# A four-layer graph kernel: layer 3 in row chunks, loads from SyncE, sums moved between engines, another planned order

## The chip, the cores and the metric

The kernel runs on one core of a Trainium2 chip. Times are microseconds (us) of device time, from the program's start to its end on that core. The kernel before took 3013.47 us as the median of three runs (3012.79 to 3015.4). One further execution was taken by the hardware profiler; it took 3013.04 us, of which the profile's span (first to last instruction) is 3011.3 us.

The engines are PE (TensorE: matmuls and transposes), DVE (VectorE), ACT (ScalarE), POOL (GpSimd) and SP (SyncE). Each works through its own queue in order. SP does nothing here but start transfers (DMAs). POOL starts the transfers that add into their target.

## The reference

There are 32 graphs of 512 nodes, 256 features each, with a weighted adjacency matrix of 512 x 512. Each graph goes through four layers, and after each layer the features are added to the layer's result and normalised by row. All values are float32.

```python
x = norm(x + L0(x, adj))    # h = (1+eps)*x + adj@x ; relu(h@W1+b1)@W2+b2
x = norm(x + L1(x, adj))    # 4 heads: softmax(leaky_relu(e_dst+e_src), masked adj>0.5) @ h + bias
x = norm(x + L2(x, adj))    # 8 heads: softmax(q@k.T/sqrt(32) + log(adj+1e-6)) @ v, then @Wo.T+bo
x = norm(x + L3(x, mask, adj))  # softmax((x@W)@x.T * adj, masked nodes) @ x
```

## The kernel before

The work of one graph is cut into a few hundred named steps, each on one engine. A node's 512 rows are four chunks of 128 (`NC` = 4), the 256 features two (`DC` = 2). The names that matter below, in order of a graph's way:

- **Loads and layer 0.** SP starts the load of `x` (512 KB, step `ldx`) and then of the whole adjacency matrix `A` (1 MB, `ldA`). PE transposes `A` in 16 blocks, one output column block m at a time (`at`, L639), so each `at` step reads all four row chunks. ACT copies each to `AT` (`ate`, L647); DVE makes the diagonal blocks with 1+eps added, `ATd` (L643). Then `hT` (L671), `h1T` with W1 (L694), `y` with W2 (L713), the residual sum (L601), and the norm: two statistics per chunk on DVE (L559, L560), `ve` (L572), a power on POOL (`rstd`, L577), `shift` (L582), and one ACT pass per chunk (L590).
- **Layer 1.** `xT` (L739), values `v` (L760), then small exponentials `R`, `S`, `T`, `nT`. `R` is transposed (L799), copied to rows (L804), written to DRAM by SP (L809) and read back spread over all partitions as one 1 MB transfer `R_bc` (L811). ACT and DVE make the weights `z` from it (L850, L861). `o1` multiplies them with the values (L884), with 64-column tiles of the PE array. Column sums of the values for nodes without edges, `hs`, are four matmuls with one column each (L822). The sums of the weights over the nodes: POOL starts transfers that add the four chunks of each head's `z` together (L912, two after each other per head), then PE multiplies by ones with 32-column tiles, 128x512 (`d1`, L930). ACT copies the sum `dT` (L941), and PE transposes both halves of the result and `dT` per chunk (`yt`: L949, L950, L951). DVE takes four small reciprocals (L957) and divides (L959).
- **Layer 2.** `q`, `k`, `v` (L1009, L1027), scores for four heads at once in 32-row tiles (`s`, L1046), exponentials (L1059), times `AT` (L1068), product with the values in 32-column tiles (`n`, L1104). The sums go as in layer 1: transfers that add (L1079, three for each half of the heads, the last behind the other two), then ones (`d2`, L1128), copy (L1136), reciprocal (`rc`, L1143), product (`yd`, L1147), output projection `p` (L1176), norm.
- **Layer 3.** `A` is loaded again as one 1 MB transfer (L1190), `iT` (L1215), scores `s` (`t`, L1229), product with `A` (`ta`, L1243), masked maximum (`tb`, L1249), exponential (`te`, L1257), all into one tile `z`. The 16 transposes (`u`, L1274) each take one block of every row chunk's `z`. Then the copies (`ue`, L1283), the product with `x` (`w`, L1301), the sum (L1315), statistics, norm, and one 512 KB store (`out`, L1330).

The weights are loaded at the start from ACT's queue (L320), 15 transfers in all, ahead of ACT's first own instruction.

The order on every engine is written by a small planner, `Plan`, while the program is built. Each step has an engine, an estimated time, the steps it comes after and the buffers it takes (`take`) and gives back (`free`). `Plan.order` walks through time: of the steps that could start soonest it picks the one with the earliest due time. A step's due time is `max(g - 1, 0) * period - left`, where `left` is the estimated time from the step to its graph's end; `stay` adds a penalty for a change between PE's tile shapes (`mode`: none, 32-row, 32-column, 64-column), of the size in the table `CHANGE`; `moved` shifts the due times of the first and the last graph's steps at random by a seed. `run` tries three settings and emits the instructions of the best. Up to six graphs are open at a time, so PE always has steps of several graphs to pick from; once emitted, the order is fixed, and an engine waits wherever the next instruction in its queue isn't ready. SP's steps count 0.1 us, and each load has a queue name of its own (`q0`, `q2`, `q3`).

Of the kernel before, what the change touches and what calls it, by code (L numbers as in the profile page):

```python
# [17 lines left out]
P = 128  # L18
# [28 lines left out]
class Plan:  # L47
# [7 lines left out]

    HOP = {"pe": 0.2, "act": 0.15, "dve": 0.13, "pool": 0.05, "sp": 0.05}
# [3 lines left out]
        "": {"": 0.0, "row": 0.1, "c32": 0.1, "c64": 0.1},  # L60
        "row": {"": 0.13, "row": 0.1, "c32": 0.2, "c64": 0.2},
# [72 lines left out]
    def order(self, period, ahead, window, stay, shift=0.0, seed=0):  # L134
# [10 lines left out]
        rng = random.Random(seed)  # L145
        moved = {n: rng.uniform(-shift, shift) for n in [*self.steps[0], *self.steps[-1]]}
# [10 lines left out]
        while low < len(self.steps):  # L157
            found = []
            for (g, name), t in ready.items():
                s = self.steps[g][name]  # L160
                t = max(t, engine.get(s.eng, 0.0))
                change = self.CHANGE[mode][s.mode] if s.eng == "pe" else 0.0
                for k, (kind, _, rest) in enumerate(s.take):
                    r, n = room[kind], sum(b[0] == kind for b in s.take[:k])
                    if len(r) <= rest + n:
                        break
                    t = max(t, r[n][0])
                else:
                    due = max(g - 1, 0) * period - self.left[g][name] + moved[name] + stay * change
                    found.append((t, due, g, name, change))  # L170
# [46 lines left out]
def fast_path(  # L217
# [57 lines left out]
    wg_sb = const.tile([P, DC, VW], F32, name="wg_sb")  # L275
    ab_off = const.tile([P, 2, H1], F32, name="ab_off")
# [6 lines left out]
    def blk(i):  # L283
# [4 lines left out]
        "B": 14, "C": 13, "p": 8,  # L288

        "live": 6, "L0": 1, "L1": 2, "L2": 2, "L3": 1, "AT": 4, "zs": 7,  # L290
        "ATd": 1, "edge": 1, "dT": 1, "tmp": 2, "rdT": 2, "node": 1,
# [7 lines left out]
    def row(name, n):  # L299
        return tuple(f"{name}{i}" for i in range(n))  # L300


    def prepare():
# [10 lines left out]
        def load(name, us, *transfers, take=()):  # L314


            @step(f"ld_{name}", "act", 0.5 * len(transfers), take=take)
            def _():
                for transfer in transfers:
                    nc.scalar.dma_start(*transfer())  # L320

            @step(name, "q3", us, (f"ld_{name}",))
            def _():
                pass
# [4 lines left out]
        def transposed(name, w):  # L329
# [4 lines left out]
            load(f"raw{name}", 1.2, raw, take=(f"C=raw{name}",))  # L334
# [18 lines left out]
        load("eps", 2.0, lambda: (eps_bc, row_bcast(eps0, 1)))  # L353
# [3 lines left out]
        def _():  # L357
# [3 lines left out]
        load(  # L361
            "w1", 3.0, lambda: (w1_sb, rows(w1)), lambda: (b1_sb, b1.rearrange("(c p) -> p c", p=P))
        )
# [8 lines left out]
        load("bias", 3.0, *(bias_rows(k, b) for k, b in enumerate((b2, gbias, bo))))  # L372

        def vector(name, a):
# [6 lines left out]
        load(  # L381
            "wg", 3.0,
            lambda: (wg_sb[:, :, :D], wg.rearrange("(c p) h f -> p c (h f)", p=P)),
            vector("a0", a_src), vector("a1", a_dst), take=("C=a0", "C=a1"),
        )

        @step("wa", "dve", 3.2, ("wg",), take=("C=prod",), free=("prod", "a0", "a1"))
        def _():
            for k in range(2):
# [6 lines left out]
                )  # L396

# [125 lines left out]
    def graph(g):  # L523
        plan.graph()
        slot = plan.slot[-1]
        t = {"g": g}
# [4 lines left out]
        def mid(key, shape, name):  # L531
            return sb.tile(shape, F32, tag=f"C{slot[key]}", name=f"{name}_{g}")

# [24 lines left out]
        def norm_stats(n, c):  # L558
            nc.vector.bn_stats(t[f"st{n}"][:, c, :], t["x"][:, c, :])  # L559
# [6 lines left out]
        def norm_steps(n, after):  # L566


            @step(f"ve{n}", "dve", 0.09, after)
            def _():  # L570
                t["ve"] = little([P, NC], f"ve{n}")
                nc.vector.tensor_scalar_add(t["ve"], t[f"mv{n}"][:, :, 1], LN_EPS)  # L572

            @step(f"dev{n}", "pool", 1.1, (f"ve{n}",))
            def _():
                t["rstd"] = little([P, NC], f"rstd{n}")
                nc.gpsimd.tensor_tensor(t["rstd"], t["ve"], nhalf, ALU.pow)  # L577

            @step(f"sh{n}", "dve", 0.09, (f"dev{n}",))
            def _():  # L580
                t["shift"] = little([P, NC], f"shift{n}")
                nc.vector.scalar_tensor_tensor(  # L582
                    t["shift"], t[f"mv{n}"][:, :, 0], -1.0, t["rstd"], op0=ALU.mult, op1=ALU.mult
                )

            for c in range(NC):

                @step(f"r{n}{c}", "act", 0.49, (f"sh{n}",) + prev(f"r{n}", c))
                def _(c=c):
                    nc.scalar.activation(  # L590
                        t["x"][:, c, :], t["x"][:, c, :], AF.Identity,
                        bias=t["shift"][:, c : c + 1], scale=t["rstd"][:, c : c + 1],
                    )
# [17 lines left out]
        @step("ldx", "sp", 0.1, take=("live", "C=x/2"))  # L611
# [4 lines left out]
        @step("ldA", "sp", 0.1, ("ldx",), take=("L0", "B=A0/5"))  # L616
        def _():
            t["A"] = big("A0", [P, NC, N], "A")
            nc.sync.dma_start(t["A"], adj[g].rearrange("(c p) m -> p c m", p=P))

        @step("ld", "q0", 8.0, ("ldA",))
        def _():
            pass


        for m in range(NC):

            @step(
                f"at{m}", "pe", 0.44, ("ld",) + prev("at", m),
                take=(f"p=at{m}",) + (() if m else ("AT=ATcap", "B=AT/5", "ATd")),  # L630
            )
            def _(m=m):
                if m == 0:
                    t["AT"] = big("AT", [P, NC, N], "AT")

                    t["ATd"] = sb.tile([P, NC, P], F32, tag="ATd", name=f"ATd_{g}")
                pt = t[f"pt{m}"] = bank(f"at{m}", [P, N], f"AT_t_{m}")
                for c in range(NC):
                    nc.tensor.transpose(pt[:, blk(c)], t["A"][:, c, blk(m)], ident)  # L639

            @step(f"atd{m}", "dve", 0.2, (f"at{m}", "^selfw"))
            def _(m=m):
                nc.vector.tensor_add(t["ATd"][:, m, :], t[f"pt{m}"][:, blk(m)], selfw)  # L643

            @step(f"ate{m}", "act", 0.52, (f"at{m}",))
            def _(m=m):
                nc.scalar.copy(t["AT"][:, m, :], t[f"pt{m}"])  # L647

            plan.free(f"at{m}", (f"atd{m}", f"ate{m}"))
        plan.free("A0", row("at", NC))  # L650
        plan.free("L0", row("at", NC))

        for d in range(DC):

            @step(
                f"h{d}", "pe", 3.49, row("ate", NC) + row("atd", NC) + prev("h", d),
# [26 lines left out]
        for f in range(HC):  # L683

            @step(
                f"f{f}", "pe", 1.72, row("he", DC) + prev("f", f) + ("^w1",),
# [33 lines left out]
        norm_steps(1, row("st1", NC))  # L720
# [6 lines left out]
        for d in range(DC):  # L727
# [5 lines left out]
            def _(d=d):  # L733
                if d == 0:
                    t["xT"] = mid("xT1", [P, DC, N], "xT1")
                    t["xs"] = little([P, DC], "xs")
# [43 lines left out]
        def _():  # L780
            t["R"] = little([P, H1 * NC], "R")
            nc.scalar.activation(
                t["R"], t["ab"][:, 1].rearrange("p h c -> p (h c)"), AF.Exp, scale=1 - SLOPE
# [13 lines left out]
        def _():  # L797
            t["pr"] = bank("Rt", [P, P], "R_t")
            nc.tensor.transpose(t["pr"][: H1 * NC, :], t["R"], ident)  # L799

        @step("Re", "dve", 0.19, ("Rt",), free=("Rt",))
        def _():
            t["Rr"] = little([H1 * NC, P], "R_rows", 1)
            nc.vector.tensor_copy(t["Rr"], t["pr"][: H1 * NC, :])  # L804

        @step("Rd", "sp", 0.1, ("Re",), take=("B=R/4",))
        def _():
            R_dram = dram.tile([H1 * NC, P], F32, tag="R_dram", name=f"R_dram_{g}")
            nc.sync.dma_start(R_dram, t["Rr"])  # L809
            R_bc = t["Rbc"] = big("R", [P, H1, N], "R_bc")  # L810
            nc.sync.dma_start(R_bc.rearrange("p h n -> p (h n)"), row_bcast(R_dram, H1 * N))  # L811

        @step("Rl", None, 8.5, ("Rd",))
        def _():
            pass

        @step("hs", "pe", 0.9, row("xe1", DC) + ("^wa",), take=("p=hs",))
        def _():
            ph = t["phs"] = bank("hs", [P, DC], "hs_ps")
            for o in range(DC):  # L820
                for d in range(DC):
                    nc.tensor.matmul(  # L822
                        ph[:, o : o + 1], wg_sb[:, d, blk(o)], t["xs"][:, d : d + 1],
                        start=(d == 0), stop=(d == DC - 1),
                    )

        @step("hse", "act", 0.1, ("hs",), free=("hs",))
        def _():
            t["hs"] = little([P, DC], "hs")
            nc.scalar.mul(t["hs"], t["phs"], TINY)  # L830
# [12 lines left out]
        for h in range(H1):  # L843
            for c in range(NC):

                @step(f"z{h}{c}", "act", 0.7, ("Rl", "ST") + prev(f"z{h}", c), take=() if c else (f"B=z{h}",))
                def _(h=h, c=c):
                    if c == 0:
                        t[f"e{h}"] = big(f"z{h}", [P, NC, N], f"z1_{h}")
                    nc.scalar.activation(  # L850
                        t[f"e{h}"][:, c, :], t["Rbc"][:, h, :], AF.Relu,
# [14 lines left out]
        plan.free("R", tuple(f"z{h}{NC-1}" for h in range(H1)))  # L866


        for hp in range(H1 // 2):
            for k in range(2):  # L870
# [20 lines left out]
                f"oe{hp}", "act", 0.59, (f"o1{hp}1", "hse") + prev("oe", hp),  # L891
# [34 lines left out]
        @step("d1", "pe", 0.87, tuple(f"as{h}1" for h in range(H1)), take=("p=d1",), mode="c32")  # L926
        def _():
            t["pd"] = bank("d1", [P, N], "d1_ps")
# [885 lines left out]
```

## Time and profile before

| | |
|---|---|
| median of three runs | 3013.47 us |
| profiled execution | 3013.04 us |
| its span | 3011.3 us |
| PE busy | 2944.1 us (98%), 15053 matmul records |
| DVE, ACT, POOL busy | 2009.7 (67%), 1946.5 (65%), 619.8 us (21%) |
| DMA queue of the adding transfers (q0) | 62.0% of the 16 engines' span |
| DMA queue of SP (q1) | 13.8% |
| first matmul of layer 3's last product, graph 16 to graph 17 | 90.53 us apart, and the same for most neighbours |

A matmul of float32 leaves two records, a transpose one. The page's groups give the busy time and the mean latency of one record; matmuls overlap in the array, so what one costs PE's queue is read from the starts of the groups that follow each other in the timeline, not from the latency. A wait names what ended last before the instruction could start. The clock line gives the share of full speed that TensorE was granted.

### The profile page before, as it was taken

The page shows a single profiled execution, that of the slowest core. Times are in us where ns is not written, and L with a number is a line of the kernel's source. Part 1 is how long each engine was busy: PE and PEld are TensorE (multiplying, and loading weights), DVE is VectorE, ACT ScalarE, POOL GpSimd, SP SyncE. Part 2 cuts the span into 40 slices and gives each one's busy share as a digit, 9 for nine tenths or more (in the row PEclk, how much of TensorE's full clock was granted, in tenths as well). Part 3 has the DMA queues.
Part 4 walks back from the last instruction along what each step waited for, and adds up shares of the span by engine and source line. Part 5 has one row for each costly group of instructions (what it writes and reads, how often), then busy time and mean ns, then how long its engine had stood idle before and what let it go on. Part 6 is the DMA issues. An engine that isn't in the chain of part 4 may idle for free. (4 is left out here: it accounts for less than half of the span.)

```text
span 3011.3 us, 40812 instructions
## 1 busy us (share of the span) xinstructions
PE 2944.1 (98%) x15053; PEld 1703.7 (57%) x15053; DVE 2009.7 (67%) x3935; ACT 1946.5 (65%) x3849; POOL 619.8 (21%) x686
## 2 busy tenths in 40 slices
PE   7899999999999999999999999999999999999996
PEld 5544655555565555565555565555565555565544
DVE  1467576676676676676676676676676676676874
ACT  2667566767666767666767666767666767666762
POOL 0222122112222112222112222112222112222210
PEclk9999999999999999999999999999999999999998
DMA  4579767788887788887787887787877787887963
GB/s 152 125 173 194 154 137 172 160 180 177 180 168 165 161 182 174 180 166 170 160 184 171 181 166 168 160 187 168 180 163 173 160 189 168 177 168 150 199 133 79
DMA packets 159782, 500.82 MB, mean 166 GB/s; under 512 B 13132, under 2 KB 48728, under 8 KB 130904
## 3 DMA queue, kind: packets, MB, share of 16 engines
q0 software_dynamic: 78336, 352.36, 62.0%
q1 hardware_dynamic: 77824, 142.88, 13.8%
q10 hardware_dynamic: 3416, 2.90, 0.3%
q8 instruction: 121, 1.98, 0.3%
q14 instruction: 85, 0.70, 0.1%
HBM read 179.06 MB, written 17.05 MB: 65 GB/s over the span
## 5 line engine op out<-in xcount | busy, mean ns | idle before, releaser
L1068 DVE SCALAR_TENSOR_TENSOR z<-AT,z 128x1024 f32<-128x1024 f32 x512 | 610.9, 1217 | 273.2 <-ACT z L1059 272.7
L1059 ACT ACTIVATE z<-s 128x512 f32<-128x512 f32 x1024 | 551.3, 611 | 268.3 <-PE s L1046 268.1
L1143 DVE RECIPROCAL rdT<-rdT 128x256 f32<-128x256 f32 x128 | 218.3, 1728 | 316.2 <-ACT rdT L1136 316.2
L861 DVE SCALAR_TENSOR_TENSOR z<-z,T,edge 128x512 f32<-128x512 f32 x512 | 357.8, 747 | 62.2 <-ACT z L850 62.0
L850 ACT ACTIVATE z<-R_bc,nT,S 128x512 f32<-128x512 f32 x512 | 382.1, 819 | 17.8 <-DMA R_bc<-R_dram 17.8
L1079 POOL DMA_DIRECT2D z<-z x192 | 169.5, 883 | 992.2 <-PE o_ps L1104 268.7
L590 ACT ACTIVATE x<-x,shift,rstd 128x256 f32<-128x256 f32 x512 | 295.4, 602 | 108.0 <-DVE shift L582 108.0
L912 POOL DMA_DIRECT2D z<-z x256 | 228.8, 1033 | 467.5 <-DMA z<-z 265.2
L1046 PE MATMUL s<-qT,kT 32*128 32x512 f32 x2048 | 291.8, 634 | 0.1
L577 POOL TENSOR_TENSOR rstd<-ve,nhalf 128x4 f32<-128x4 f32 x128 | 134.7, 1052 | 696.9 <-DVE ve L572 671.6
L1104 PE MATMUL o_ps<-z,v 128*32 128x512 f32 x2048 | 260.5, 601 | 0.3 <-ACT z L1059 0.3
L694 PE MATMUL h1T_ps<-hT,w_sb 128*128 128x512 f32 x512 | 240.0, 604 | 0.0
L1229 PE MATMUL s<-xT,iT 128*128 128x512 f32 x512 | 237.4, 598 | 0.0
L1301 PE MATMUL o_ps<-x,eT 128*128 128x256 f32 x1024 | 237.4, 385 | 0.0
L713 PE MATMUL y_ps<-w_sb,h1T 128*128 128x256 f32 x1024 | 232.4, 381 | 2.2 <-ACT h1T L700 2.2
L884 PE MATMUL o_ps<-z,v 128*64 128x512 f32 x1024 | 230.8, 602 | 1.5 <-DVE z L861 1.5
L1301 PEld LDWEIGHTS o_ps<-x,eT 128*128 128x128 f32 x1024 | 189.5, 190 | 68.1 <-issue 22.8
L713 PEld LDWEIGHTS y_ps<-w_sb,h1T 128*128 128x128 f32 x1024 | 194.6, 191 | 52.8 <-issue 20.7
L671 PE MATMUL hT_ps<-AT,x 128*128 128x384 f32 (+2 forms) x768 | 210.1, 383 | 8.8 <-ACT AT L647 8.8
L559 DVE BATCH_NORM_STATS2 st<-x 128x6 f32<-128x256 f32 x512 | 211.9, 414 | 5.6
L1046 PEld LDWEIGHTS s<-qT,kT 32*128 32x128 f32 x2048 | 93.5, 183 | 158.7 <-issue 66.8
L694 PEld LDWEIGHTS h1T_ps<-hT,w_sb 128*128 128x128 f32 x512 | 90.5, 190 | 122.0 <-issue 112.8
(145 smaller groups left out, 4261.5 us busy)
## 6 DMA issues: line engine op xcount, KB each, us to landing
z<-z POOLq DMA_DIRECT2D x192, 1024.0 KB, 8.2
A<-in_adj_dram SPq DMA_DIRECT2D x64, 1024.0 KB, 11.0
z<-z POOLq DMA_DIRECT2D x128, 512.0 KB, 8.0
x<-biases POOLq DMA_DIRECT2D x96, 512.0 KB, 9.6
R_bc<-R_dram SPq DMA_DIRECT2D x32, 1024.0 KB, 4.5
z<-z POOLq DMA_DIRECT2D x128, 256.0 KB, 7.7
x<-in_x_dram SPq DMA_DIRECT2D x32, 512.0 KB, 6.0
out_dram<-x SPq DMA_DIRECT2D x32, 512.0 KB, 3.8
```

Of the source, the lines that this page charges most:

```text
L590: nc.scalar.activation(t["x"][:, c, :], t["x"][:, c, :], AF.Identity, bias=t["shift"][:, c : c + 1], scale=t["rstd"][:, c : c + 1],)
L694: nc.tensor.matmul(ph, w1_sb[:, d, blk(f)], t["hT"][:, d, :], start=(d == 0), stop=(d == DC - 1))
L713: nc.tensor.matmul(py[:, j, :], t["h1T"][:, f, blk(2 * c2 + j)], w2_sb[:, f, :], start=(f == 0), stop=(f == HC - 1),)
L850: nc.scalar.activation(t[f"e{h}"][:, c, :], t["Rbc"][:, h, :], AF.Relu, bias=t["nT"][:, h, c : c + 1], scale=t["S"][:, h, c : c + 1],)
L861: nc.vector.scalar_tensor_tensor(z, z, t["T"][:, h, c : c + 1], t["edge"][:, c, :], op0=ALU.add, op1=ALU.mult)
L884: nc.tensor.matmul(po[j * F1 : (j + 1) * F1, :], t["v"][:, c, h * F1 : (h + 1) * F1], t[f"e{h}"][:, c, :], start=(c == 0), stop=(c == NC - 1),
L1046: nc.tensor.matmul(pk, t["k"][hs, o, blk(c)], t["q"][hs, o, :], start=True, stop=True)
L1059: nc.scalar.activation(t[f"E{k}"][:, j, :], t[f"ps{k}{j}"], AF.Exp, scale=QSCALE)
L1068: nc.vector.scalar_tensor_tensor(z, t["AT"][:, c, None, :].to_broadcast([P, 2, N]), ADJ_EPS, z, op0=ALU.add, op1=ALU.mult,)
L1104: nc.tensor.matmul(t[f"n{o}"][32 * j : 32 * j + 32, :], t["v2"][:, c, o * P + F2 * j : o * P + F2 * (j + 1)], t[f"E{k}"][:, j, :], start=( ...
L1229: nc.tensor.matmul(pt, t["iT"][:, d, blk(c)], t["xT3"][:, d, :], start=(d == 0), stop=(d == DC - 1),)
L1301: nc.tensor.matmul(py[:, j, :], t["eT"][:, m, blk(2 * c2 + j)], t["x"][:, m, :], start=(m == 0), stop=(m == NC - 1),)
```

## The change

The change rewrites many steps and the settings of the planner. By part:

1. **Start.** `A` is loaded in four row chunks, ahead of `x`. `at` now takes one row chunk and writes one block column of `AT` (a strided copy). The large weights go to SP's queue behind the first graph's `A` and `x`; only `eps`, `b1`, the biases and `a_src`/`a_dst` stay with ACT.
2. **Layer 1.** `R_bc` becomes four transfers, one per head. The feature sums `xs` travel as two more columns of `R` through the same transpose and DRAM write, are read back by all partitions, and DVE makes `hs` from them with two reductions against a transposed `wg` (made once, `wtg`, `weg`). The four `hs` matmuls go. `d1` multiplies by `pick`, a 128x32 matrix with a column of ones at place c, 16 matmuls of 128 columns that leave the sums as [32h + c, node]; one transpose (`dt`) and one reciprocal (`rd1`) then serve all four chunks, and `yt` transposes two blocks instead of three.
3. **Layer 3 by row chunks.** `A`, `z` and `eT` become strips of 256 KB, and scores, mask, exponential, transpose, copy, product run chunk by chunk; the transposes of a chunk no longer wait for the other chunks.
4. **Last graph.** For graph 31 alone layer 2's sums are made by PE over all chunks (32 matmuls instead of 8, and no adding transfers), and the last norm and the store run per chunk. `yd` is split in halves for every graph.
5. **Planner.** SP's steps count 0.45 us and share a transfer queue `q1`; buffers are regrouped into 19 strips (`D`); `CHANGE` has other numbers; every step's due time can be shifted, by a list of seeds found beforehand; one setting is left.

```diff
-        "": {"": 0.0, "row": 0.1, "c32": 0.1, "c64": 0.1},
-        "row": {"": 0.13, "row": 0.1, "c32": 0.2, "c64": 0.2},
+        "": {"": 0.0, "row": 0.13, "c32": 0.1, "c64": 0.1},
+        "row": {"": 0.17, "row": 0.1, "c32": 0.2, "c64": 0.2},
...
+        for seed, far in shifts:
+            rng = random.Random(seed)
+            for n in moved:
+                if rng.random() < 0.15:
+                    moved[n] += rng.uniform(-far, far)
...
+    pick = const.tile([P, NC, 32], F32, name="pick")
+    nc.gpsimd.memset(pick, 0.0)
+    for c in range(NC):
+        nc.gpsimd.memset(pick[:, c, c : c + 1], 1.0)
...
+    def transfer(name, us, after, queue="q1"):
+        @step(f"{name}.q", queue, us, after)
+        def _():
+            pass
+        @step(name, None, 2.0, (f"{name}.q",))
+        def _():
+            pass
...
-                    nc.scalar.dma_start(*transfer())
+                    (nc.scalar if little else nc.sync).dma_start(*transfer())
...
+                t[f"A{c}"] = strip(f"A0{c}", [P, N], f"A{c}")
+                nc.sync.dma_start(t[f"A{c}"], adj[g].rearrange("(c p) m -> p c m", p=P)[:, c, :])
...
-                for c in range(NC):
-                    nc.tensor.transpose(pt[:, blk(c)], t["A"][:, c, blk(m)], ident)
+                for m in range(NC):
+                    nc.tensor.transpose(pt[:, m, :], t[f"A{c}"][:, blk(m)], ident)
...
-                nc.scalar.copy(t["AT"][:, m, :], t[f"pt{m}"])
+                nc.scalar.copy(t["AT"][:, :, blk(c)], t[f"pt{c}"])
...
-            nc.sync.dma_start(R_bc.rearrange("p h n -> p (h n)"), row_bcast(R_dram, H1 * N))
+                nc.sync.dma_start(t[f"R{h}"], row_bcast(t["Rdram"][h * NC : (h + 1) * NC, :], N))
...
-                    nc.tensor.matmul(
-                        ph[:, o : o + 1], wg_sb[:, d, blk(o)], t["xs"][:, d : d + 1],
-                        start=(d == 0), stop=(d == DC - 1),
-                    )
+                nc.vector.tensor_tensor_reduce(
+                    t["xsr"][:, 1, :], t["xsr"][:, 0, :], wgT[:, o, :], TINY, 0.0,
+                    op0=ALU.mult, op1=ALU.add, accum_out=t["hs"][:, o : o + 1],
+                )
...
-                nc.tensor.matmul(
-                    t["pd"][32 * h : 32 * h + 32, :], ones[:, :32], t[f"e{h}"][:, 0, :],
-                    start=True, stop=True,
-                )
+            for c in range(NC):
+                for h in range(H1):
+                    nc.tensor.matmul(
+                        t["pd"][32 * h : 32 * h + 32, :], pick[:, c, :], t[f"e{h}"][:, 0, blk(c)],
+                        start=(c == 0), stop=(c == NC - 1),
+                    )
...
-                nc.tensor.transpose(pt[:, 2, :], t["dT"][:, blk(c)], ident)
...
-            if c % 2:
+            if c % 2 and not last:
                 collect(k, k - 1, (f"n{k-1}", f"m{k}1"))
...
-            @step(f"u{m}", "pe", 0.44, row("te", NC) + prev("u", m), take=(f"p=u{m}",))
+            @step(f"u{c}", "pe", 0.44, (f"te{c}",) + prev("u", c), take=(f"p=u{c}",), free=(f"z3{c}",))
...
-        norm_steps(4, row("st4", NC))
+        norm_steps(4, [[c] for c in range(NC)] if last else [range(NC)])
...
-        plan.run([(28, 0.0, 6, 100.0, 8.0, 34035), (28, 0.05, 6, 30.0, 3.0, 427523), (28, 0.0, 6, 15.0)])
+        plan.run([(33, 0.0, 6, 55.0, ((619770, 10.0), ...), (0.7, 0.0, 0.0))])
```

In the order that comes out, PE's queue repeats from graph to graph as it did before, with 21 changes of tile shape per graph in both kernels. On POOL, the power of layer 2's norm of one graph now stands behind three of the four second adding transfers of layer 1 of the next graph but one. The last 35 groups of PE's queue mix graphs 30 and 31, and graph 31's layer 3 stands alone at the end.

## The prediction

> **What bounds the kernel now.** I read the page's busy shares first: PE 98%, no other engine over 67%. Then PE by stretches of the span, to see where the missing 2% lies (columns: stretch, its length, busy us of PE, of weight loads, DVE, ACT, POOL, clock, DMA share, GB/s).
>
> ```profile
> 0.00:11.60 11.60, 0.00 (x0) 0.03 (x1) 1.01 (x8) 0.00 (x0) 0.96 (x10) 1.00 0.76 249
> 11.60:32.47 20.87, 12.04 (x56) 10.20 (x57) 1.17 (x4) 3.92 (x6) 0.00 (x0) 1.00 0.81 277
> 470.00:2650.00 2180.00, 2179.93 (x11274) 1268.10 (x11275) 1504.18 (x2937) 1465.81 (x2894) 460.01 (x504) 1.00 0.79 171
> 2957.30:2998.70 41.40, 30.35 (x99) 18.57 (x100) 17.29 (x43) 12.39 (x25) 2.04 (x2) 0.84 0.04 13
> 2998.70:3011.30 12.60, 1.25 (x6) 0.76 (x4) 4.02 (x14) 2.07 (x4) 1.01 (x1) 0.70 0.14 46
> ```
>
> From 470 to 2650 us PE never waits: a graph takes 90.53 us there because its matmuls do. All 67.2 us in which PE is idle lie at the ends: 20.4 before 32 us, 17.3 more up to 470, 16.9 from 2841 to 2998.7, 12.6 after the last matmul. So only two things can move the time: fewer microseconds in PE's queue per graph (times 32), and shorter ends. PE's own waits (us in total, times, longest) and the timeline of ACT name the first gaps:
>
> ```profile
> PE AT_t L639 <- DMA A<-in_adj_dram: 11.6, 1, 11.6
> PE hT_ps L671 <- ACT AT L647: 8.8, 1, 8.8
> ```
>
> ```profile
> 22.58 1.28 ACT L647 ACT_TABLE_LOAD   x1 [22.58 <-DMA a<-in_L_gnn_a_dst_dram]
> ```
>
> PE waits for all of `A`, then for ACT's copies, and ACT is still starting weight loads until 22.6 us. The chain that ended last gives the other end (start, us, what):
>
> ```profile
> 2934.05 12.76 DMA z<-z
> ...
> 2947.34 10.10 DMA z<-z
> ...
> 2964.08 6.07 PE o2p_ps L1176 x14
> ```
>
> The last graph's weight sums wait for two adding transfers in a row; after the sums PE waits 4.8 us for DVE's reciprocal, and the projection, 3.45 us at full clock, takes 6.07 for 14 of its 16 records. Prices in PE's queue come from starts of neighbours in a steady stretch of the timeline (start, us of the group with its latency):
>
> ```profile
> 1583.17 0.95 PE L822 MATMUL hs_ps<-xs,wg_sb 128*128 128x1 f32 x8
> 1584.05 7.09 PE L884 MATMUL o_ps<-z,v 128*64 128x512 f32 x32
> ...
> 1612.41 1.04 PE L930 MATMUL d_ps<-z,ones 128*32 128x512 f32 x8
> 1613.39 0.66 PE L639 MATMUL AT_t<-ident,A 128*128 128x128 f32 x4
> ...
> 1616.10 0.27 PE L949 MATMUL y_t<-ident,yT 128*128 128x128 f32 x1
> 1616.21 0.27 PE L950 MATMUL y_t<-ident,yT 128*128 128x128 f32 x1
> ```
>
> So `hs` costs 0.88, `d1` 0.98, a transpose 0.109.
>
> **What the Trainium skill says.** "TensorE: Matmul & The Clock Gate", section "What's actually happening": after an idle window of about 3.4 us the array runs at half clock until it has been busy for one. The trace agrees: stretches of 3.4 us or two or three times that at 0.5 begin at 85, 130, 201, 263, 471, 2922, 2963 and 2973 us, most just after a gap; 44 us in all, so a gap costs more than itself. The same page, "Part 3", "The mechanism": matmuls on different tiles run together, starting about 4 ns apart; in `d1` I see four starting 7 ns apart. "LDWEIGHTS (loading the stationary operand)": the load takes columns/1.2 ns, 27 ns for 32 columns; the trace shows 109 ns for one with its latency. "DMA: Bandwidth & Descriptors", "Anatomy of one DMA": 2 us plus bytes at 436 GB/s; `R_bc` (1 MB) gives 4.4 us, and its median in the trace is 4.5.
>
> **The change, part by part** (against the profiled execution; its span is 3011.3 us, its time 3013.04, 0.4 under the median).
>
> *PE's queue, every graph.* `hs` leaves: -0.88. `yt` loses four transposes and `dt` adds one: -3 x 0.109 = -0.33. `d1` becomes 16 matmuls of two records: eight rounds of four tiles with 128 columns. A round costs 0.107 us if the weights load under the round before, as a round of 512 columns does now (429 ns): 0.86 plus the 0.11 of leaving the tile shape, 0.97 as before. If no load is covered, a round is 0.107 + 0.109 and `d1` 1.84, +0.86. I take +0.05, since the loads of a round start together. The other matmuls are the same in number and shape, and both orders change tile shape 21 times per graph, at some 0.1 us each. Sum -1.16 per graph, 89.4 instead of 90.5; over 32 graphs -37.
>
> *Waits in the steady part.* Now none; these edits move work onto DVE (two reductions of 256 columns, some 0.5 each by the 0.42 of L559 and the 0.08 read-out, less three reciprocals of 0.17 and plus three for `rd3`: +1.0 of 62.8 us per graph), and SP starts 17 transfers per graph, at 0.33 to 0.45 some 7 us of 90. Both lie in idle time. I walked the new order with the old durations for the closest waits. (a) From `dt` to the next transposes of layer 2, PE has 13.2 us of other work. Behind it stand, on DVE, `tb` 0.75, four times 0.43 + 0.42 + 0.42 + 0.18, small ones, to about 8.1; then ve, power, shift 1.7, ACT 2.1, hand-overs 0.2: 12.1. Cover 1.1. (b) `R` to `o1`: 25 us for some 16, and its landing is spread from 4.2 to 9.3. (c) Fifth `n` of layer 2: its weights are ready within 0.2 us of its turn. (d) Layer 2's norm: PE leaves 8.6 us after the projection, the chain takes 5.6, cover 3.0; but its power is behind three second adds on POOL. In the timeline of POOL before:
>
> ```profile
> 1586.30 3.59 POOL L912 DMA_DIRECT2D z<-z  x4 [5.09 <-PE o_ps L884]
> 1591.31 0.86 POOL L912 DMA_DIRECT2D z<-z  x1 [1.42 <-DMA z<-z]
> 1598.34 0.86 POOL L912 DMA_DIRECT2D z<-z  x1 [6.17 <-DMA z<-z]
> 1600.94 1.75 POOL L912 DMA_DIRECT2D z<-z  x2 [1.74 <-DMA z<-z]
> ```
>
> The third second add goes out 14.6 us after the first add; that puts the power some 1 us late, under the cover. No wait is forced, several are near: I take 0.3 us per graph, from 0 to 1, over 28 graphs +8.
>
> *Start.* By 11.6 us the engines had moved 2.9 MB; `A` now needs its 1 MB alone, about 6.5 us. ACT starts 7 transfers, at 0.5 and one 1.5 about 5.3 us; it stood still 2.1 and 3.7 us among such before, so 5.3 to 10. Then table 1.28 and four copies 2.05: first `hT` at 8.6 to 13.5, I take 11.5, against 24.5, of which 0.6 was done ahead: -12.4. W1 and W2 stand behind `x` on SP and have 7 us of `hT` to land.
>
> *Rest of the filling, 32 to 470 us.* 17.3 us idle, up to 13.6 lost to half clock. `z` of the first graph still bounds `o1` (16 ACT passes of 0.75 after `R`): about 4 of idle stay. The rest depends on where the order put other graphs' steps; I take half: -10 (0 to -20).
>
> *Drain.* Graph 31 needs no adding transfers: its two sums cost 24 more matmuls at 0.215, +5.2, and the 23 us of transfers go. PE had other work under most of those. Left idle: graph 30's own sums, the reciprocal, `n` behind DVE's queue near the end, the norm: about 9 of 16.9, and less half clock: -12 + 5.2 = -6.8. Layer 3 by chunks also removes the 1.8 us before the transposes there; in mid-run these were covered.
>
> *End.* Now 12.6: 7.5 from the last product to the store's start, 5.1 after. For one chunk: 0.46 + 0.32 + 0.18 + 0.18 + 1.02 + 0.17 + 0.6 + hand-overs 0.2 = 3.1, and a store a quarter as large, about 4.2: -5.3. `wtg`: +0.4.
>
> Sum: -37 + 8 - 12.4 - 10 - 6.8 - 5.3 + 0.4 = -63: span 2948, time **2950 us**.
>
> **Rivals.** *A wait per graph of about 1 us.* One of (a), (c), (d), or uncovered weights in `d1`. For: covers are thin. Against: the old order has the same kind of thin covers, and 2180 us without a wait. 0.7 to 0.9 more than taken, times 28: about 2973. *The ends go clean:* no steady wait (-8), start at 9 (-2.5), filling at its best (-10): 2930. *Slower:* POOL's power of layer 2's norm. If the adds land later than now (7.8 median, 19.7 longest in the trace), it is late by as much less the 2 us of cover left, every graph, and DVE's shift and ACT's passes with it. It takes 2.5 us per graph to eat the gain; 3.5 gives 3040. Against: the adds are no more and no larger, and queue 0 stays at 62%. *The change does nothing:* PE's sums as now and ends traded; it can't be in the matmul count, only in a wait of 2.5 us, so about 3013.
>
> **How the numbers follow.** Likeliest 0.60 (its own range 2935 to 2966); wait 0.19; clean 0.10; slower 0.08; nothing 0.03. The range 2928 to 2990 holds the first, nearly all of the second and half of the clean case. A change of 0.2% is about what runs of this kernel can tell from none. Faster by more: 0.89; within: 0.03; slower: 0.08.
>
> **What would show it.** In the profile after: 89.4 to 89.7 us from graph to graph; no PE wait over 0.5 us between 450 and 2750; `d_ps` groups 0.9 to 1.1 apart from the next; first `hT` near 11 us; under 8 us after the last matmul; fewer half-clock stretches. Wrong would be: a wait of layer 2's or 3's transposes for ACT's norm passes in every graph, or `d1` near 1.8.

## The result, and the profile after

The changed kernel takes 3012.78 us (median, 3008.11 to 3015.3), the kernel before 3014.43 beside it: 0.9993 of it, 95% interval 0.9975 to 1.001. No difference can be told. The forecast was 2950. The profiled execution has a span of 3008.2 us and a time of 3010.3.

PE by stretches of the span, kernel after (columns as in the prediction):

```profile
0.00:8.70 8.70, 3.64 (x16) 3.27 (x16) 1.30 (x9) 1.47 (x2) 1.30 (x15) 1.00 0.67 222
...
470.00:2650.00 2180.00, 2148.50 (x11413) 1238.75 (x11415) 1513.74 (x3025) 1415.42 (x2810) 458.85 (x495) 1.00 0.79 170
...
2853.00:3000.10 147.10, 138.76 (x728) 70.57 (x726) 106.48 (x209) 83.86 (x169) 20.93 (x24) 0.98 0.45 98
3000.10:3008.20 8.10, 0.02 (x1) 0.00 (x0) 1.44 (x6) 1.20 (x2) 0.84 (x2) 0.66 0.19 56
```

Before, PE was idle for 67.2 us, nearly all of it at the ends. Now the ends have 35.5 (8.2 up to 32.5 us, 10.9 up to 470, 8.3 from 2853, 8.1 after the last product) and the middle, which had none, has 34.2. The ends became shorter as forecast, and the steady part gave it back: from one graph's first `w` product to the next it is 92.4 us (mean of 23 graphs, 91.6 to 94.5), where it was 90.53 every time and 89.4 was forecast.

What PE waits for, kernel after (us in total, times, longest):

```profile
PE h1T_ps L747 <- ACT hT L731: 22.9, 24, 2.2
PE o_ps L946 <- ACT z L1129: 13.0, 15, 2.1
PE AT_t L691 <- DMA A<-in_adj_dram: 6.3, 2, 5.0
```

Two waits recur, both for ACT: `f` (the product `h1T` with W1, L747) for the copy of `hT`, 24 times over 32 graphs, and layer 1's product `o1` for a PSUM bank that ACT's exponentials (exps) of layer 2 free, 15 times. A third one isn't in this view. Start-to-start times of the products, summed by step over 23 graphs, show it (us per graph):

| step | before | after |
|---|---|---|
| `s`, layer 2 scores | 8.35 | 9.33 |
| `o1`, layer 1's product | 7.02 | 7.96 |
| `f` | 7.36 | 8.05 |
| `hs` | 0.88 | 0 |
| `d1` | 0.97 | 0.90 |
| `yt` and `dt` | 1.31 | 0.98 |

`s` has the same 64 records. The timelines of PE, before and then after, show where it loses one us (start, us of the group, engine, line):

```profile
1592.92 2.00 PE L1046 MATMUL s<-qT,kT 32*128 32x512 f32 x16
```

```profile
1837.50 1.12 PE L747 MATMUL h1T_ps<-hT,w_sb 128*128 128x512 f32 x2 [0.92 <-ACT hT L731]
...
1841.99 2.98 PE L1116 MATMUL s<-qT,kT 32*128 32x512 f32 x16
1844.90 1.94 PE L946 MATMUL o_ps<-z,v 128*64 128x512 f32 x8
1847.02 1.94 PE L946 MATMUL o_ps<-z,v 128*64 128x512 f32 x8 [0.18 <-ACT z L1129]
```

Sixteen score records (eight products) take 2.98 us instead of 2.00, and no idle time is shown. The four products of a round run on four tiles. In the second round two start at 1842.96. The third starts at 1843.27, just after ACT's copy of `kT` (L1085) has ended at 1843.22, the fourth at 1843.85, just after ACT's L753 has ended at 1843.80. All four read the same part of `kT`, so what the two wait for is most likely the banks that these two instructions give back. Meanwhile the others keep PE busy in the records.

One graph of the changed kernel by the timelines of SP and POOL, then ACT, then DVE, shows what is late:

```profile
1818.44 0.29 SPq L863 DMA_DIRECT2D R_dram<-R_rows  x1
1823.21 1.94 SPq L872 DMA_DIRECT2D R_bc<-R_dram  x4
1825.26 0.39 SPq L880 DMA_DIRECT2D xs_row<-R_dram  x1
```

```profile
1815.94 0.93 POOL L1149 DMA_DIRECT2D z<-z  x1
1821.51 0.87 POOL L583 DMA_DIRECT2D x<-biases  x1 [4.64 <-ACT xT L1064]
```

```profile
1828.38 0.81 ACT L911 ACTIVATE z<-R_bc,nT,S 128x512 f32<-128x512 f32 x1 [5.75 <-DMA R_bc<-R_dram]
...
1836.88 0.57 ACT L731 COPY hT<-hT_ps 128x512 f32<-128x512 f32 x1
...
1842.63 0.58 ACT L1085 COPY kT<-kT_ps 128x512 f32<-128x512 f32 x1
...
1845.89 0.60 ACT L637 ACTIVATE x<-x,shift,rstd 128x256 f32<-128x256 f32 x1 [1.61 <-DVE shift L627]
```

```profile
1831.48 0.43 DVE L888 CUSTOM_DVE_ANT_0 xs_row<-xs_row,wgT 128x256 f32<-128x256 f32 x1 [7.33 <-DMA xs_row<-R_dram]
...
1832.30 6.71 DVE L922 SCALAR_TENSOR_TENSOR z<-z,T,edge 128x512 f32<-128x512 f32 x10
```

POOL starts the last adding transfer of layer 2's weight sums (L1149, 1 MB, of the graph two before) at 1815.94, and SP starts `R`'s write, 9 KB, 2.5 us later. The write's first packet goes at 1822.44, as the adding transfer's last ones do; the four strips start 4.77 us after the write. They meet the bias transfer of L583, and the first `z` pass comes 9.94 us after the write. The plan of the changed kernel had put it 6.0 after. DMA packets by queue (count, MB, share of the 16 engines) from 1815.9 to 1822.3 us, up to just before the write's first packet (q8 is one packet of instructions):

```profile
q0 software_dynamic: 178, 1.18, 92.7%
q8 instruction: 1, 0.02, 0.9%
```

Before, the write fell where queue 0 was empty:

```profile
1632.70 0.33 SPq L809 DMA_DIRECT2D R_dram<-R_rows  x1
1634.12 0.33 SPq L811 DMA_DIRECT2D R_bc<-R_dram  x1
```

That is only part of the difference. In the kernel before, the first `z` pass came 9.1 us after the write (one transfer of 1 MB has to land first), and nothing waited. What shrank is the room behind it. There, `o1` of the graph whose write is at 1632.70 starts 41.9 us later:

```profile
1674.58 7.09 PE L884 MATMUL o_ps<-z,v 128*64 128x512 f32 x32
```

In the changed order it is 26.5 us from the write at 1818.44 to `o1` at 1844.90, and 24.3 in the runs below in which nothing waits.

Two things hang on this landing. On ACT, `hT`'s and `kT`'s copies stand among the sixteen late `z` passes, and `f` and `s` wait for them. On DVE, the two reductions for `hs` stand ahead of all the products of `z` (L922) and wait 7.33 us for `xs_row`; behind those products stand layer 3's sum and norm, ACT waits 1.61 us for the norm's `shift`, and behind ACT's waiting pass stand the exps that free `o1`'s bank.

### The profile page after: what moved, and what is told of

Read it like the earlier page. It is cut to its first block, busy times and chain, and to the rows that moved or that the text cites. A ratio compares the mean times of both kernels' runs of the same rounds, so it can differ in the third digit from the quotient of the medians.

```text
span 3008.2 us, 42752 instructions
## 1 busy us (share of the span) xinstructions
PE 2938.5 (98%) x15521; PEld 1687.7 (56%) x15521; DVE 2060.2 (68%) x4133; ACT 1928.2 (64%) x3818; POOL 626.8 (21%) x688
## 3 DMA queue, kind: packets, MB, share of 16 engines
q0 software_dynamic: 77472, 346.06, 60.4%
q1 hardware_dynamic: 101648, 149.75, 15.5%
## 4 chain that ended last, share of the span: by engine, by line
PE 73%; DVE 10%; DMA 9%; ACT 5%; issue 2%; POOL 1%; SPq 0%; ACTq 0%; POOLq 0%; DVEq 0%
PE s L1317 8%; PE o_ps L1174 7%; PE s L1116 7%; PE y_ps L766 7%; PE o_ps L946 6%; DVE z L922 5%; PE o_ps L1371 5%; PE iT_ps L1303 4%; PE h1T_ps L747 4%; PE v_ps L815 4%; PE o2p_ps L1259 4%; ACT z L911 4%; PE v_ps L1097 4%; DMA xs_row<-R_dram 3%; DMA R_bc<-R_dram 3%; PE qT_ps L1079 2%
## 5 line engine op out<-in xcount | busy, mean ns | idle before, releaser
L1129 ACT ACTIVATE z<-s 128x512 f32<-128x512 f32 x1024 | 566.1, 602 | 126.9 <-PE s L1116 123.0
L911 ACT ACTIVATE z<-R_bc,nT,S 128x512 f32<-128x512 f32 x512 | 380.0, 809 | 181.7 <-DMA R_bc<-R_dram 181.6
L637 ACT ACTIVATE x<-x,shift,rstd 128x256 f32<-128x256 f32 x508 | 283.2, 592 | 127.9 <-DVE shift L627 127.8
L922 DVE SCALAR_TENSOR_TENSOR z<-z,T,edge 128x512 f32<-128x512 f32 x512 | 350.4, 746 | 10.7 <-ACT z L911 10.2
L1149 POOL DMA_DIRECT2D z<-z x186 | 165.9, 901 | 787.5 <-DVE z L1138 337.6
L1116 PE MATMUL s<-qT,kT 32*128 32x512 f32 x2048 | 313.3, 638 | 2.1 <-ACT qT L1085 2.1
L619 POOL TENSOR_TENSOR rstd<-ve,nhalf 128x4 f32<-128x4 f32 (+1 forms) x131 | 161.3, 1232 | 682.9 <-DVE ve L613 634.3
L747 PE MATMUL h1T_ps<-hT,w_sb 128*128 128x512 f32 x512 | 243.0, 599 | 23.2 <-ACT hT L731 22.9
L946 PE MATMUL o_ps<-z,v 128*64 128x512 f32 x1024 | 244.9, 608 | 17.4 <-ACT z L1129 13.0
L766 PE MATMUL y_ps<-w_sb,h1T 128*128 128x256 f32 x1024 | 226.2, 379 | 0.0
L1116 PEld LDWEIGHTS s<-qT,kT 32*128 32x128 f32 x2048 | 103.6, 183 | 199.9 <-ACT z L1129 68.0
L583 POOL DMA_DIRECT2D x<-biases x96 | 86.0, 897 | 584.0 <-PE hT_ps L724 294.2
```

Of the source, the lines that this page charges most:

```text
L637: nc.scalar.activation(xn, xn, AF.Identity, bias=t[f"shift{n}"][:, c : c + 1], scale=t[f"rstd{n}"][:, c : c + 1],)
L747: nc.tensor.matmul(ph, w1_sb[:, d, blk(f)], t["hT"][:, d, :], start=(d == 0), stop=(d == DC - 1))
L766: nc.tensor.matmul(py[:, j, :], t["h1T"][:, f, blk(2 * c2 + j)], w2_sb[:, f, :], start=(f == 0), stop=(f == HC - 1),)
L911: nc.scalar.activation(t[f"e{h}"][:, c, :], t[f"R{h}"], AF.Relu, bias=t["nT"][:, h, c : c + 1], scale=t["S"][:, h, c : c + 1],)
L922: nc.vector.scalar_tensor_tensor(z, z, t["T"][:, h, c : c + 1], t["edge"][:, c, :], op0=ALU.add, op1=ALU.mult)
L946: nc.tensor.matmul(po[j * F1 : (j + 1) * F1, :], t["v"][:, c, h * F1 : (h + 1) * F1], t[f"e{h}"][:, c, :], start=(c == 0), stop=(c == NC - 1),
```

## The experiments

Where steps are moved, the plan and its buffers stay as they are and one list is edited between plan and emission. A move names a step, how many graphs further its anchor is, the anchor, and the side: 1 is later, just behind it; -1 and -2 are earlier, just ahead of it and just behind it. That adds 13 lines, so L911 is L924 in those profiles.

```diff
-        for g, name, _, got in self.order(*best[1])[1]:
+        seq = self.order(*best[1])[1]
+        for name, dg, anchor, side in self.moves:
+            for g in range(1, len(self.steps)):
...
+                    seq.insert(j, seq.pop(k))
+        for g, name, _, got in seq:
```

All results. Times are medians, intervals 95% against the kernel before. "Period" is the mean of 23 graphs; the last two columns are medians over 22 graphs from the start of `R`'s write to the first `z` pass and to the first product of `z` on DVE:

| kernel | us | ratio | period | z | product |
|---|---|---|---|---|---|
| before | 3014 | 1 | 90.53 | 9.1 | 10.6 |
| after | 3012.8 | 0.9975 to 1.001 | 92.42 | 10.1 | 13.9 |
| add_later | 3010.5 | 0.9967 to 1.0004 | 92.18 | 4.8 | 14.0 |
| hsl_later | 3014.3 | 0.9989 to 1.0007 | 92.37 | 9.9 | 10.7 |
| add_hsl (both) | **2932.9** | 0.971 to 0.9742 | 89.69 | 4.6 | 5.6 |
| all3 | 2972.8 | 0.9842 to 0.9875 | 90.71 | 4.7 | 5.6 |
| he_first | 3022.8 | 1.0016 to 1.0043 | 92.53 | 10.0 | 14.0 |
| r_const | 2997.5 | 0.9932 to 0.9965 | 91.89 | 7.2 | 13.6 |
| r_const_hsl | 2963.4 | 0.982 to 0.9853 | 90.58 | 7.3 | 8.1 |
| hs_on_pe | 3026.8 | 1.0026 to 1.0055 | 92.90 | 10.1 | 10.9 |
| add_hs_on_pe | 2950.4 | 0.9778 to 0.9811 | 90.37 | 4.7 | 5.6 |
| before_nohs | 2991.3 | 0.991 to 0.9943 | 89.74 | – | – |
| replan1 | 3072.1 | 1.0166 to 1.0201 | 95.27 | 15.9 | 16.8 |
| replan3 | 2964.8 | 0.9813 to 0.9846 | 90.75 | 12.3 | 13.2 |

**The adding transfer behind the bias transfer (add_later).** `cd6` is the transfer of L1149 above, `xd3` the bias transfer of L583. The expectation calls `cd6` layer 3's; it is layer 2's.

```diff
+    moves = [('cd6', 1, 'xd3', 1)]
```

> The changed kernel with one step moved in POOL's queue: layer 3's last adding transfer of each graph (L1149, for the second value sum) starts behind the bias transfer (L583) instead of ahead of it. Theory A (R is late because its rows are written to DRAM behind that adding transfer): from the write's start to the first R_bc's start 1.3 to 2 us instead of 4.8, first z pass 2 to 4 us earlier after R's write, PE's waits for hT (22.9 us in total) nearly gone and those for the o_ps banks smaller, period 90 to 91 instead of 92.4, time 2945 to 2975. Theory B (ACT's own queue is too long for PE's order, and the landing of R only shows in it): z starts earlier, but the waits for hT and for the banks stay, time 3005 to 3015.

Measured: the strips start 1.31 us after the write instead of 4.82, `z` after 4.8 instead of 10.1, and the wait for `hT` is gone from the steady part, as theory A had it. The time is not what A forecast: 3010.5, the median of 20 executions from 2988.6 to 3027.8. The wait moved to `o1`'s banks (PE's waits of this run), and DVE's timeline says why:

```profile
PE o_ps L959 <- ACT z L1142: 38.6, 20, 2.3
```

```profile
1836.28 0.42 DVE L901 CUSTOM_DVE_ANT_0 xs_row<-xs_row,wgT 128x256 f32<-128x256 f32 x1 [9.29 <-DMA xs_row<-R_dram]
```

`xs_row` starts 3.2 us after the write but lands only 15 us after it, behind the bias and the adding transfer that now follow; the reductions hold DVE until then. Not in every graph: in the profiled execution 6 of 23 graphs take 89.5 us, as if nothing waited, and the others up to 96.4. In seven of these PE also has stretches at half clock, 27.3 us in all against 6.8 in the changed kernel; by an estimate from these lengths, half of each, this takes some 14 us of the run instead of 3. Theory A fell as a whole cause, and theory B, whose time came true, has the wrong reason: DVE, not ACT's length. So theory C was formed: two chains are late, `R` to `z` on ACT and `xs_row` to the products on DVE, and they end in the same place.

**hT's copies earlier in ACT's queue (he_first).**

```diff
+    moves = [('he0', -1, 'z20', -1), ('he1', 0, 'h1', -2)]
```

> The changed kernel with two steps moved in ACT's queue: the two hT copies of each graph (L731) stand ahead of the third and behind the seventh of the sixteen z passes instead of behind the sixth and the eleventh. R stays late. Theory A (z late, everything behind z late): PE's wait for hT (0.8 us per graph) goes, the staggered s rounds and the bank waits of o_ps (together some 1.8 us per graph) stay or take over part of it: time 2985 to 3005. Theory B (ACT's queue order alone costs the waits): hT's wait goes and the later ones shrink with it, 2950 to 2985. If neither: the s rounds take over the whole, 3010.

Measured 3022.8: slower. `f` takes 7.58 instead of 8.05 per graph, `s` 9.91 instead of 9.33: what is put ahead of the late `z` passes is paid for by what stands behind them. (In the queue that came out, the copies stand behind the second and the sixth pass.) So the place of `hT`'s copies among the passes isn't the cause; other orders on ACT weren't tried.

**R's strips without the write (r_const).** What is computed is then not layer 1's attention.

```diff
-row_bcast(t["Rdram"][h * NC : (h + 1) * NC, :], N)
+row_bcast(x[g][2 * h : 2 * h + 2, :], N)
```

> The changed kernel with R's strips read from rows of x instead of from the rows that were just written, so the four R_bc transfers no longer wait for the write to land (what the output then is isn't R's; bytes, transfers and passes are the same). The write and xs_row stay. Theory A (late R): strips start 3.5 to 4 us earlier but still stand behind the adding transfer in the engines, so z starts 2 to 4 us earlier, period 90 to 91.5, time 2950 to 2985. Theory B (ACT's length): no change, 3005 to 3015.

Measured 2997.5, 15 us less than the changed kernel, between the two forecasts. `z` starts 2.9 us earlier, `f`'s wait nearly goes (4.2 us in all), the products on DVE still start after 13.6, and the bank waits grow to 44.7 us. The same shift as in add_later, without touching POOL.

**The reductions behind the products on DVE (hsl_later), both moves (add_hsl), and hT's copies on top (all3).**

```diff
+    moves = [('hsl', 0, 'zm21', 1)]
```

> The changed kernel with one step moved in DVE's queue: the two reductions for hs (L888) stand behind twelve... of the z products (just behind the product of head 2's second half) instead of ahead of all sixteen. R stays late. Theory C (DVE stands still at the reductions until xs_row lands, and with it the products, layer 3's norm, ACT's passes and exps behind that norm, and so PE's banks): the products start when the second pass of head 0 ends, about where they start now because z itself is late, but 1 us of reductions leaves the path: o_ps bank waits and staggered s rounds fall by 0.5 to 1 us per graph, hT's wait stays at 0.8: time 2975 to 3000. Theory A alone (only R's landing counts): 3005 to 3015.

> Both moves: layer 3's last adding transfer behind the bias transfer on POOL, and hs's reductions behind the products on DVE. Theory C: z starts 4.7 us after R's write and the products at 9 to 10 instead of 15.8, layer 3's norm ends some 5 us earlier, ACT's exps wait for nothing, bank waits near 0, period 89.3 to 90, time 2925 to 2950. Theory A or B alone: no better than the first move by itself, 3000 to 3015.

> The two moves of add_hsl and the hT copies earlier in ACT's queue. Theory C: hT was not late any more with z early, so the same as add_hsl within 5 us, 2925 to 2950. If ACT's order still costs: up to 15 us better than add_hsl.

The reductions now stand behind fourteen of the sixteen products. hsl_later alone: nothing, 3014.3, against 2975 to 3000 expected (it falls into the range written for theory A). The products do start 3.2 us earlier, but `z` is as late as in the changed kernel, so `f` (8.09), `s` (9.33) and `o1` (7.92) lose what they lost. Both moves: 2932.9, 80 us under the changed kernel and 2.7% under the kernel before. One move gains 2, the other -1, the two together 80: each chain alone is enough to hold PE in most graphs. DVE shows where the chains meet. Its tenth product, with layer 3's sum and norm next in the queue, ends 20.65 us after the write in the changed kernel, 20.66 with the adding transfer moved, 20.2 with the reductions moved and 16.0 with both (medians of 22 graphs). With `z` late the products wait for ACT; with `z` early they wait behind the reductions. The timelines of PE and then ACT for one graph with both moves:

```profile
1793.48 2.00 PE L1129 MATMUL s<-qT,kT 32*128 32x512 f32 x16
1795.40 3.65 PE L959 MATMUL o_ps<-z,v 128*64 128x512 f32 x16
```

```profile
1775.78 1.52 ACT L924 ACTIVATE z<-R_bc,nT,S 128x512 f32<-128x512 f32 x2 [0.48 <-DMA R_bc<-R_dram]
...
1795.13 0.59 ACT L650 ACTIVATE x<-x,shift,rstd 128x256 f32<-128x256 f32 x1
```

The scores are back at 2.00 us, `o1` runs through, and ACT's pass no longer waits for DVE's `shift`. By stretches PE is busy for all of 470 to 2400 us, and again from 2420 to 2650. In between, one graph has a late strip, PE waits 2.2 us for `hT` and then has 3.4 us at half clock, and that graph takes 94.05 us:

```profile
470.00:2400.00 1930.00, 1930.00 (x10437) 1121.83 (x10436) 1386.29 (x2760) 1309.15 (x2573) 423.00 (x452) 1.00 0.81 175
```

`f`, `s` and `o1` take 7.09, 8.39 and 7.17 us per graph there, 2.69 less than in the changed kernel, and the period is 2.73 shorter: those three steps are nearly the whole of it. The granted clock doesn't explain it: 0.996 in both. With hT's copies earlier on top, 2972.8, 40 us worse where the same or better was expected: `s` and `o1` lose 0.4 and 0.8 again, and the tenth product ends at 18.8. PE's waits name ACT's exps for `o1`, 28 times; which passes ahead of them made them late wasn't traced. So the order on ACT does cost once `R` is early.

**Early R without moving POOL's transfers (r_const_hsl).**

> R's strips read from rows of x (so they don't wait for the write; what is computed is then not R's) and hs's reductions behind the products on DVE; POOL's queue as in the changed kernel. If the two late chains (R to z on ACT, xs_row to the products on DVE) are the cause, and not something else that moving the adding transfer does, this gives most of what both moves gave: products start about 8 us after R's write, bank waits nearly gone, period 89.5 to 90.3, time 2930 to 2955. If the adding transfer's place matters for another reason (the weight sums or A's landing): 2980 to 3000.

Measured 2963.4, between the two forecasts, with `z` 7.3 us after the write and 13.6 us of bank waits left. With the reductions out of the way the time follows `z`: 9.9 us after the write gives 3014.3, 7.3 gives 2963.4, 4.6 gives 2932.9. So with POOL's queue untouched `R`'s lateness alone accounts for 51 of the 81 us. The other 30 fit the same line, but no run keeps them apart from what else moving the adding transfer does.

**hs back on PE (hs_on_pe), the same with R early (add_hs_on_pe), and hs left out of the kernel before (before_nohs).** In the first two the eight matmuls write into the bank of `R`'s transpose; `xs_row` and the reductions are gone.

```diff
+                    nc.tensor.matmul(
+                        t["pr"][:, P + o : P + o + 1], wg_sb[:, d, blk(o)], t["xs"][:, d : d + 1],
+                        start=(d == 0), stop=(d == DC - 1),
...
-            nc.sync.dma_start(t["xsr"][:, 0, :], row_bcast(t["Rdram"][H1 * NC :, :], D))
...
-                nc.vector.tensor_tensor_reduce(
```

> The changed kernel with one part undone: hs by eight matmuls on PE again (behind R's transpose, in its bank), no xs_row transfer and no reductions on DVE; R's write starts some 0.8 us later. If PE's sum were what it says, the edit was worth 0.88 us per graph, and undoing it costs 28 us: 3040. Theory C: undoing it also frees DVE, so the bank waits fall by about as much: 3000 to 3020.

> The adding transfer behind the bias transfer on POOL, and hs on PE again (no xs_row, no reductions on DVE). Nothing is late then, so PE's sum alone must set the period: 0.88 us more per graph than with both moves, 90.4, and 28 us more in all: 2955 to 2965. If the reductions on DVE or xs_row cost something even when they wait for nothing, undoing them costs less than 28: 2933 to 2950. If the hs matmuls, which stand ahead of R's write, make R late again: over 2970.

> The kernel before without the eight hs matmuls on PE (left out: hs is then xs times the small constant). Same order for all the rest. If PE's queue bounds the steady part as the prediction took it, the period falls by 0.88 us, 90.5 to 89.6, and the time by about 28 us, to 2985. If the kernel before is as close to another limit (ACT, the adding transfers), 3000 to 3013.

Undoing the edit in the changed kernel costs 14 us, between the two forecasts and half of what PE's sum says: PE gets its 0.88 back, and `o1` takes 7.49 instead of 7.96 with DVE free (products 3 us earlier). Undoing it where nothing is late costs 17.5 us (2950.4, at the edge of the second forecast); the undisturbed graphs take 90.27 instead of 89.49, +0.78, which would be 25 over 32 graphs. The 23 graphs in the middle account for 15.5 of it; the nine at the ends, where PE has idle time, for little. Left out of the kernel before it brings 23.5 us, 0.79 per graph. So the edit is worth some 0.8 per graph when nothing waits for it.

**Planned anew (replan1, replan3).** The plan knew the adding transfers on one queue and SP's on another, side by side. Here `R`'s write, its strips and `xs_row` are put on the queue of the adding ones (the first of three such lines is shown), and the order is searched again with other seeds.

```diff
-        transfer("Rs", 0.2, ("Rsi",))
+        transfer("Rs", 0.2, ("Rsi",), "qa")
```

> The changed kernel, planned anew: the plan puts R's write, its four strips and xs_row on the same queue as the adding transfers, as they are in the engines, and the order is searched again with that. Planned z 10.3 us after R's write (6.0 in the changed kernel's plan, 10.05 measured there). If the plan's one wrong assumption was that queue, an order made with it keeps PE busy with R late: period 89.2 to 90, time 2920 to 2950. If other durations of the plan are wrong by as much: waits elsewhere, 2960 to 3010.

> The same with another order that the search found (planned z 11.0 us after R's write, the reductions 16.5). As for the other: 2920 to 2955 if the queue was the plan's one wrong assumption, 2960 to 3010 if not.

Measured 3072.1 and 2964.8: the first above both of its ranges, the second in the range written for other wrong durations. The first had planned `z` 10.3 us after the write and got it after 15.9; PE then waits for `hT` in every graph:

```profile
PE h1T_ps L747 <- ACT hT L731: 66.1, 23, 2.9
```

After these waits TensorE runs at half clock for 3.4 or 6.8 us in 19 of 23 graphs, 89 us in all; half of that, some 44 us by an estimate from these lengths, is most of the 59 us by which replan1 is slower than the changed kernel. So the shared queue was not the plan's one wrong assumption: even with it, `z` comes 1 to 6 us later than planned. What else the plan has wrong stays open.

## Why the prediction was wrong, step by step

- *PE's queue, every graph* (-1.16): right. With nothing waiting it is 89.49 instead of 90.53, -1.04. `hs` was worth 0.79 rather than 0.88, `yt` and `dt` -0.33 as said; some 0.15 came back in other products. `d1` takes 0.90, not 0.98 + 0.05: its 32 short records cost less than the eight long ones. Its rounds start 0.109 us apart, so the weight loads run under the round before. The lines are 0.90 us apart:

```profile
1877.50 1.08 PE L994 MATMUL d_ps<-z,pick 128*32 128x128 f32 x32
1878.40 1.04 PE L1174 MATMUL o_ps<-z,v 128*32 128x512 f32 x8
```

- *Start* (-12.4): right. First product at 4.99 us, PE's idle time up to 32 us 8.2 instead of 20.4.
- *Rest of the filling* (-10, 0 to -20): right, at the better end: 10.9 us idle instead of 17.3, and 6.8 us at half clock instead of 23.9.
- *Drain* (-6.8): right in kind. Idle time up to the last product's end is 8.3 instead of 18.0 (the forecast read 16.9); no adding transfer is in the chain, and the sums are `d_ps` groups of 32.
- *End* (-5.3): too large. From the last product to the end it is 8.1 us; before it was 11.3, and the 12.6 of the forecast held 1.25 us of products. -3.2.
- *Waits in the steady part* (+0.3 per graph, +8): **this step failed.** Measured about 2.7 per graph, 80 us in all: the difference of the changed kernel to add_hsl. Its item (b) compared 25 us from `R` to `o1` with "some 16" and took the landing from the kernel before. The 25 was right (24.3 with nothing waiting). The 16 can be held against the tenth of the sixteen products: it ends 16.0 us after the write with both moves, and 20.65 in the changed kernel. In the kernel before the write met an empty queue 0 in nearly every graph, and `o1` came 41.9 us after it. In the changed order an adding transfer goes out 2.5 us ahead of it; I didn't lay POOL's and SP's queues side by side. Nor was `o1`'s own input the first thing to be late: `hT` and `kT` stand in ACT's queue behind `z`, and `f` and `s` wait for them.
- With this step's +8 taken out the forecast would be 2942; the kernel with both moves takes 2932.9. The rest of the sum was 9 us too cautious.
- In the same step, "these edits move work onto DVE ... both lie in idle time" priced the reductions by their duration (1.0 us). What cost was their place: an instruction that waits for a transfer, with ten products and a norm queued behind it. Whom they hold up wasn't asked.
- Of the four close waits, (a), (c) and (d) didn't come up among the recurring waits. (d), POOL's power behind the adds, was the slower rival: 3040 didn't come. Its "against" (the adds are no more and no larger, queue 0 at 62%) was true, 60.4%, and beside the point: it was not how full the queue is but what else stands behind it.
- The rival that fits is "the change does nothing ... only a wait of 2.5 us", at 3013, which I gave 0.03 for want of a place for such a wait. That the number came true is luck, since no wait of that size was named. The rival "a wait per graph of about 1 us" fits the kind, but not the size, and none of its candidates was the cause.
- "What would show it": first `hT` near 11 us (8.7, in a stream from 11.3), `d_ps` 0.9 apart, and fewer half-clock stretches (20 us instead of 44, up to the last product) came; 8 us after the last product was missed by 0.1; 89.4 per graph and no PE wait over 0.5 us did not, and they point to the step that failed.

## What to carry to other kernels

Don't carry a transfer's latency over from the old trace: put the queues side by side in the new order, see which large transfer starts just ahead, and how much room is left behind the landing. An instruction that waits for a transfer is priced by what is queued behind it, not by its own duration. And two late chains that meet hide each other: a fix that brings nothing alone may be half of one that brings 80 us.

## What the runs showed of the hardware

- In this kernel a small transfer on SP's queue didn't pass a large adding one from POOL's. `R`'s write has its first packet 0.82 to 0.84 us after its start in 29 of the 32 graphs of the kernel before, and 2.1 to 3.7 in the other three, which met an adding transfer. In the changed kernel it is 3.9 to 4.4 in 28 of 32, and 0.8 again in the first and the last graph, where no adding transfer is in the way. From the write's start at 1818.44 to 1822.4 us only queue 0 has packets. From the write's start to that of the transfer that waits for it, it is 1.42 us when all is quiet and 4.8 here.
- The Trainium skill, in "DMA: Bandwidth & Descriptors", "Anatomy of one DMA", gives 2 us plus the bytes' time at 436 GB/s for a transfer that GpSimd starts. For an adding transfer of 1 MB that would be 4.4 us, an estimate from this page; in the trace of the changed kernel the median of 186 such transfers, others in flight among them, is 7.8. The fit isn't meant for SP's transfers, so the write doesn't test it.
- Products of one round on four tiles can wait one by one. A lost us then lies inside a group that is longer (2.98 instead of 2.00 for sixteen score records), and in no idle time and no list of PE's waits; the records of the weight loads do show it.
- PE's short waits cost more than themselves where they were followed by half clock: 89 us at half clock in 23 graphs of replan1, with 66 us of waits for `hT` in all, against none in the same 23 graphs of the kernel before.
